# A small GpSimd write behind every fourth gather of a sparse graph attention

## The chip, the cores and the metric

The kernel runs on one core of one Trainium2 chip. The metric is the device time of one execution in microseconds (us). Lower is better. The engines are named as in the profile: PE is TensorE (PEld its weight loads), DVE is VectorE, ACT is ScalarE, POOL is GpSimd, SP is SyncE. [...]

## The reference, cut to what matters

Layer 0 is a graph attention of 8 heads over 4096 nodes with a 0/1 adjacency of about 32 neighbours per row; layer 1 takes three quantiles per feature over the kept neighbours of each node.

```python
Wh = jnp.einsum('nd,hde->hne', nodes, W)
e = leaky_relu(f1[:, :, None] + f2[:, None, :], 0.2)      # f1, f2: Wh times a1, a2
att = softmax(where(adj > 0, e, -9e15), axis=-1)
h = elu(jnp.einsum('hnm,hmd->hnd', att, Wh))
x = layernorm(nodes + elu(concat_heads(h) @ W1 + b1))
# layer 1, per node: drop some neighbours by rank, then
svals = sort(where(keep[:, :, None], x[None], big), axis=1)
agg = mean over q in (0.25, 0.5, 0.75) of svals[ceil(q * n_keep) - 1]
out = (0.5 * agg + 0.5 * x) @ W.T + b + x
```

## The kernel before, in words

The adjacency is turned into lists of neighbour indices (`neighbours`, `complete_records`), and nodes are sorted by their number of neighbours, so that a tile of 128 nodes (128 partitions) has lists of about equal length. The 32 tiles are worked in three blocks of 4, 9 and 19 tiles (`BLOCKS`). While the attention of one block runs, the lists of the next block are searched in small pieces between the attention's own instructions; the third block has no such search beside it, only the preparation of layer 1 in its last six steps. After all 32 tiles comes the quantile stage, called the sort stage below.

One call of `step` (L340) handles two tiles:

- `fetch_rows` (L818) issues the gathers of one tile. A tile has 24 to 64 slots, rounded up to a multiple of four, and each slot is one indirect DMA on POOL (`gather`, L177, recorded at L178) that brings a row of 136 floats for each of the 128 partitions. Sixteen slots share one buffer `G`, and the pool holds six of them (L829). Between the gathers stand some scatters (L187): the records of the next block, or `all_d` in the third block. `keep_x1` (L335) adds one scatter of finished rows per step.
- `attend` (L844) computes the attention of the tile before it. It is a chain over DVE, ACT and PE: logits `z` (L858, L864, exp at L865), denominators (L871, L881, L882), their spreading back (`rz`, L886, L895), block-diagonal weights `wide` of one layer of slots after another in two buffers (L902), one matmul per slot into `y` (L913), then the two dense layers in two halves of four heads (copies at L927, matmuls L934 and L948, ELU at L943, L945, L946) and the layer norm (`finish_x1`, L969). The last matmul into `y` that reads a `G` frees this buffer for later gathers.
- After the first part of `attend`, `prepare` reads the list of the next tile but one (`read_lists`, L767), whose transposed indices the next gathers need.

The order on each engine is the order in which the program issues (`manual_schedule`), and each engine takes its instructions in this order. A gather waits for its indices (DVE), for a free `G` (PE) and for the DMA that used its semaphore earlier. A matmul of L913 waits for its own gather.

Of the kernel before, what the change touches and what calls it, by code (L numbers as in the profile page):

```python
# [9 lines left out]
F32 = mybir.dt.float32  # L10
# [9 lines left out]
P = 128  # L20
# [156 lines left out]
def gather(nc, dst, rows, idx):  # L177
    nc.gpsimd.indirect_dma_start(  # L178
        out=dst,
        out_offset=None,  # L180
        in_=rows,
        in_offset=bass.IndirectOffsetOnAxis(ap=idx, axis=0),
    )


def scatter(nc, rows, src, idx):
    return nc.gpsimd.indirect_dma_start(  # L187
        out=rows,
        out_offset=bass.IndirectOffsetOnAxis(ap=idx, axis=0),
        in_=src,  # L190
        in_offset=None,
    )
# [9 lines left out]
def kernel(  # L202
# [137 lines left out]
    def step(fetch=None, soon=None, pieces=None, quota=0, first=False, among=()):  # L340
        if first:
            keep_x1(fetch)
        if fetch:
            weigh.append(fetch_rows(tc, attp, fetch, xt_d, list(among)))
        if not first:
            keep_x1(fetch)
        if len(weigh) > 1 or (weigh and not fetch):
            done = 0
            each = quota / STEPS
            for k, x1_t in enumerate(attend(tc, attp, pp, weigh.pop(0), consts)):  # L350
                if soon:
                    ready.append(prepare(*soon))
                    soon = None
                while done < min(quota, (k + 1) * each):
                    next(pieces, None)
                    done += 1
            store.append(x1_t)
            quota -= done
        if soon:
            ready.append(prepare(*soon))  # L360
        for _ in range(quota):
            next(pieces, None)
# [455 lines left out]
def fetch_rows(tc, ap, lists, xt_d, among):  # L818

    nc = tc.nc  # L820
    R, mine, parts = lists
    out = []
    left = sum(w for _, w, _, _ in parts)
    G, col = None, 16
    for s0, w, idx, f1v in parts:
        runs = []
        for g in range(w):
            if col == 16:
                G, col = ap.tile([P, 16, XW], F32, name="G", bufs=6), 0  # L829
            if not runs or col == 0:  # L830
                runs.append([G, col, g, 0])
            runs[-1][3] += 1
            gather(nc, G[:, col, :], xt_d, idx[:, g : g + 1])
            col += 1
            left -= 1
            if among and left % 2 == 0 and left <= 2 * len(among) + 4:
                scatter(nc, *among.pop(0))
        out.append((w, P // w, runs, f1v))
    for v in among:
        scatter(nc, *v)  # L840
    return R, mine, out
# [545 lines left out]
```

## Time and profile before

| | |
|---|---|
| median of 3 runs | 3876.51 us (3872.57 to 3877.78) |
| the profiled execution, its own time | 4780.24 us, span 4778.5 us |
| mean granted TensorE clock in it | 0.563 |
| POOL busy | 2763.5 us, 58% of the span, 2388 instructions |
| DVE busy | 2676.4 us, 56% |
| PE busy | 1355.3 us, 28% |
| gathers of the attention (`G`, L178) | 1180 indirect DMAs, mean 958 ns |
| gathers of the sort stage (`vals`, L178) | 1024 indirect DMAs, mean 1390 ns |

The profiled execution is 903.7 us longer than the median of the timed runs. Times in the lines of the trace are us from the span's start. In a line of the timeline the first number is the start, the second the duration, and the bracket gives the idle time of the engine before it and what ended this idle time; "issue" means that the profile shows nothing that was waited for, "remote" that it can't name the source. In a line of the groups the number after the `|` is the busy time in us, then the mean ns of one, then the idle time before the group and what ended most of it.

The attention's first gather starts at 113.9 us and its last at 2743.7 us; the sort stage's first gather starts at 2851.3 us.

### The profile page before, as it was taken

What the parts mean: (1) busy time and instruction counts of PE and PEld (TensorE: products, weight loads), DVE (VectorE), ACT (ScalarE), POOL (GpSimd) and SP (SyncE); (2) the same over time, 40 slices, a digit from 0 to 9 for tenths busy, and PEclk for the clock granted to TensorE, in tenths of its full rate; (3) what the DMA queues carried; (4) which work ended last, traced back from release to release, by engine and by line L of the source; (5) the groups of instructions that cost most, each with busy time, mean ns of one, the idle gap of its engine ahead of it and who ended that gap; (6) DMA issues with size and microseconds to landing.
All of it is one profiled execution on the core that took longest, in us unless ns stands there. A gap on an engine that the chain in (4) does not pass through costs nothing. (4 is left out here: it accounts for less than half of the span.)

```text
span 4778.5 us, 22122 instructions
## 1 busy us (share of the span) xinstructions
PE 1355.3 (28%) x5429; PEld 1026.7 (21%) x5433; DVE 2676.4 (56%) x6455; ACT 413.3 (9%) x667; POOL 2763.5 (58%) x2388
## 2 busy tenths in 40 slices
PE   5373445556233443343424250000000000000010
PEld 2042333333232342232423240000000000000010
DVE  7463354554313111111134235687779999999868
ACT  2110111211000101100000010000000000000000
POOL 1534434334544454544444518888878888888883
PEclk9995555555555555555555555555555555555555
DMA  5321323321111111111111101111111111111110
GB/s 182 113 72 40 115 77 95 99 79 47 45 42 35 37 41 35 39 36 39 43 36 31 40 8 43 40 40 37 39 41 41 37 30 33 41 40 37 36 40 20
DMA packets 110282, 241.26 MB, mean 50 GB/s; under 512 B 46976, under 2 KB 63360, under 8 KB 101952
## 3 DMA queue, kind: packets, MB, share of 16 engines
q0 software_dynamic: 76160, 160.24, 12.5%
q10 hardware_dynamic: 9360, 67.18, 4.1%
q1 hardware_dynamic: 24624, 12.34, 1.1%
q8 instruction: 45, 0.74, 0.1%
q14 instruction: 93, 0.76, 0.1%
HBM read 228.44 MB, written 11.15 MB: 50 GB/s over the span
## 5 line engine op out<-in xcount | busy, mean ns | idle before, releaser
L178 POOL DMA_INDIRECT G<-xt_d,idx x1180 | 1130.7, 958 | 1285.2 <-issue 692.4
L178 POOL DMA_INDIRECT vals<-x_d,idx x1024 | 1423.4, 1390 | 314.5 <-issue 303.2
L1113 DVE TENSOR_TENSOR work<-work 128x256 f32<-128x256 f32 (+7 forms) x1168 | 922.0, 824 | 0.7
L913 PE MATMUL y<-wide,G 128*128 128x32 f32 (+3 forms) x2360 | 540.2, 410 | 234.2 <-DVE wide L902 137.9
L1113 DVE TENSOR_TENSOR work<-work,work 128x512 f32<-128x512 f32 (+4 forms) x820 | 584.7, 739 | 1.3
L1133 PE MATMUL st_ps<-dg,goal 128*128 128x128 f32 x286 | 71.1, 425 | 1794.4 <-DVE goal L1113 1430.9
L913 PEld LDWEIGHTS y<-wide,G 128*128 128x128 f32 x2360 | 516.8, 328 | 267.4 <-DVE wide L902 150.1
L945 DVE TENSOR_SCALAR half<-half 128x512 f32<-128x512 f32 x64 | 27.6, 432 | 915.3 <-ACT half L943 822.3
L1133 PEld LDWEIGHTS st_ps<-dg,goal 128*128 128x128 f32 x286 | 63.0, 321 | 1800.4 <-issue 1799.5
L563 DVE MAX8 first<-key 128x8 f32<-128x128 f32 x1024 | 228.0, 283 | 300.9 <-remote 132.6
L1113 DVE TENSOR_TENSOR work<-vals 128x768 f32<-128x768 f32 (+11 forms) x64 | 128.8, 2028 | 269.6 <-DMA vals<-x_d,idx 266.0
L948 PE MATMUL small<-W_sb,half 128*128 128x128 f32 x512 | 120.8, 410 | 484.7 <-DVE half L946 315.7
L596 PE MATMUL key<-sgn,markb 128*128 128x512 bf16 x255 | 151.0, 593 | 254.1 <-DVE first L563 105.0
L948 PEld LDWEIGHTS small<-W_sb,half 128*128 128x128 f32 x512 | 102.9, 298 | 503.9 <-DVE half L946 331.0
L934 PE MATMUL hT<-half,W_sb 128*128 128x128 f32 x512 | 116.1, 400 | 236.3 <-ACT half L927 143.7
L557 ACT ACTIVATE sgn<-adj_t 128x2048 bf16<-128x2048 int32 x64 | 122.1, 1907 | 555.0 <-PE key L596 387.1
L927 ACT COPY half<-y 128x512 f32<-128x512 f32 x64 | 65.5, 1023 | 1073.7 <-remote 536.5
L934 PEld LDWEIGHTS hT<-half,W_sb 128*128 128x128 f32 x512 | 103.9, 301 | 252.0 <-ACT half L927 153.6
L886 PE MATMUL rz<-rden,ownT 4*128 4x32 f32 (+3 forms) x436 | 112.3, 434 | 152.8 <-DVE rden L882 113.8
L599 PE MATMUL key<-parts,oneb 64*128 64x512 bf16 x256 | 149.1, 583 | 9.0 <-POOL parts L196 6.3
L1132 ACT ACTIVATE dg<-ident,wt 128x128 f32<-128x128 f32 x143 | 47.5, 393 | 1092.5 <-PE st_ps L1133 1008.4
L886 PEld LDWEIGHTS rz<-rden,ownT 4*128 4x128 f32 x436 | 98.4, 322 | 170.9 <-DVE rden L882 124.6
(178 smaller groups left out, 1773.0 us busy)
## 6 DMA issues: line engine op xcount, KB each, us to landing
adj_t<-in_adj_dram ACTq DMA_DIRECT2D x64, 1024.0 KB
G<-xt_d,idx POOLq DMA_INDIRECT x1180
vals<-x_d,idx POOLq DMA_INDIRECT x1024
R<-rec_d SPq DMA_DIRECT2D x128, 26.2 KB
xt_d<-rec SPq DMA_DIRECT2D x4, 544.0 KB
rec<-in_x_dram SPq DMA_DIRECT2D x4, 512.0 KB
W_sb<-in_L_gnn_W_dram SPq DMA_DIRECT2D x2, 512.0 KB
a_b<-in_L_gnn_a_dram SPq DMA_DIRECT2D x2, 512.0 KB
```

The source lines that it names most:

```text
L178: nc.gpsimd.indirect_dma_start(out=dst, out_offset=None, in_=rows, in_offset=bass.IndirectOffsetOnAxis(ap=idx, axis=0),)
L557: nc.scalar.activation(sgn, adj_t, AF.Sign, accum_out=cnt[:, i : i + 1])
L563: nc.vector.max(first[:, ts(c0 // CW + c, 8)], key[:, ts(c, CW)])
L596: nc.tensor.matmul(key, lhsT=markb, rhs=sgn[:, ts(b, 512)], start=True, stop=False)
L599: nc.tensor.matmul(key, lhsT=oneb[0:64, :], rhs=parts[:, ts(r, 512)], start=False, stop=True)
L886: nc.tensor.matmul(rz[:, layer[i] * H : (layer[i] + w) * H], lhsT=ownT[w][:, r, :], rhs=rden.rearrange("p (g r h) -> p r g h", r=k // 4, h ...
L913: nc.tensor.matmul(yf[:, ts(g, c)], lhsT=G[:, col + g - g0, 0:D], rhs=pf[:, ts(g, c)], start=(i == 0 and g % (w // 2) == 0), stop=(i == le ...
L927: nc.scalar.copy(yT.rearrange("p h (u g) -> p g u h", u=4), yf.rearrange("p (g u h) -> p g u h", u=4, h=H)[:, :, :, h0 : h0 + 4],)
L934: nc.tensor.matmul(hT[:, ts(h, P)], lhsT=consts["W_sb"][:, h0 + h, :], rhs=yT[:, h, :], start=True, stop=True,)
L948: nc.tensor.matmul(o, lhsT=hv[:, h, :], rhs=consts["W1_sb"][:, h0 + h, :], start=(h0 + h == 0), stop=(h0 + h == H - 1),)
L1113: nc.vector.tensor_tensor(slots_of(dst, (j, c, s, m), size), slots_of(a, (i, c, s, m), size), slots_of(b, (i + d, c, s, m), size), op,)
L1133: nc.tensor.matmul(st_ps[:, u, :], lhsT=goal[:, (j * k + u) * D : (j * k + u + 1) * D], rhs=dg, start=(j == 0), stop=False,)
```

## The change

One instruction is added to the loop of `fetch_rows`: when the number of slots that are left of the tile is a multiple of four, POOL writes zeros to a tile of 128 partitions by 128 floats. The tile comes from the attention's pool with one buffer, and nothing reads it.

```diff
             gather(nc, G[:, col, :], xt_d, idx[:, g : g + 1])
             col += 1
             left -= 1
+            if left % 4 == 0:
+                nc.gpsimd.memset(ap.tile([P, 128], F32, name="pause", bufs=1), 0.0)
             if among and left % 2 == 0 and left <= 2 * len(among) + 4:
                 scatter(nc, *among.pop(0))
```

## The prediction, made before the changed kernel ran

> **What bounds the kernel now.** I read the page's second part first, for where in the span POOL is full: it is the only engine that gets added work.
>
> ```profile
> DVE  7463354554313111111134235687779999999868
> POOL 1534434334544454544444518888878888888883
> PEclk9995555555555555555555555555555555555555
> ```
>
> Up to slice 23 (the attention; the gathers run from 113.9 to 2743.7 us) POOL is busy four or five tenths of the time, in the sort stage eight. By these rows an added POOL instruction in the attention has room. But this execution took 4780.24 us, and the median of the timed runs is 3876.51 us: 903.7 us less. Where they go decides the case. The groups give POOL's work:
>
> ```profile
> L178 POOL DMA_INDIRECT G<-xt_d,idx x1180 | 1130.7, 958 | 1285.2 <-issue 692.4
> L178 POOL DMA_INDIRECT vals<-x_d,idx x1024 | 1423.4, 1390 | 314.5 <-issue 303.2
> ```
>
> The timeline of POOL shows the rhythm: 0.95 us of work, 0.30 us between, 1.25 us per gather, then a long gap to the next tile's first gather.
>
> ```profile
> 1556.73 0.94 POOL L178 DMA_INDIRECT G<-xt_d,idx  x1 [0.30 <-issue]
> 1557.98 1.00 POOL L187 DMA_INDIRECT x_d<-x_t,mine  x1 [0.30 <-issue]
> 1596.93 0.96 POOL L178 DMA_INDIRECT G<-xt_d,idx  x1 [37.95 <-issue]
> 1598.20 0.95 POOL L178 DMA_INDIRECT G<-xt_d,idx  x1 [0.30 <-issue]
> ```
>
> In the window of the gathers POOL has 1180 x 1.25 = 1475 us of them and 89 scatters x 1.31 = 117 us: 1592 of 2630 us. Some 1040 us are gaps, and these end when the chain of `attend` goes on. So I looked at the chain, in the timeline of all engines:
>
> ```profile
> 1628.21 0.37 PE L913 MATMUL y<-wide,G 128*128 128x128 f32 x1 [2.44 <-issue]
> ...
> 1642.39 1.22 DVE L902 TENSOR_TENSOR wide<-z,own 128x1024 f32<-128x1024 f32 x1 [28.34 <-remote]
> 1642.63 1.80 POOL L178 DMA_INDIRECT G<-xt_d,idx  x1 [5.12 <-remote]
> ```
>
> The third `wide` waits only until the first layer's matmuls have freed its buffer. The last recorded matmul of even the second layer ends at 1628.6 us, yet DVE, and POOL beside it, go on at 1642.4 us, released by nothing that the profile names. The timeline of ACT has more of such holds:
>
> ```profile
> 2183.63 0.44 ACT L865 ACTIVATE z<-z 128x288 f32<-128x288 f32 x1 [1.43 <-DVE z L864]
> 2212.09 1.02 ACT L927 COPY half<-y 128x512 f32<-128x512 f32 x1 [28.02 <-PE y L913]
> ...
> 2215.82 1.03 ACT L927 COPY half<-y 128x512 f32<-128x512 f32 x1
> 2244.34 0.60 ACT L943 ACTIVATE half<-hT 128x512 f32<-128x512 f32 x1 [27.49 <-issue]
> 2258.60 0.31 ACT L976 ACTIVATE ve<-v 128x128 f32<-128x128 f32 x1 [13.66 <-DVE v L974]
> ...
> 2263.43 0.44 ACT L865 ACTIVATE z<-z 128x288 f32<-128x288 f32 x1 [1.43 <-DVE z L864]
> ```
>
> ```profile
> 2761.12 0.50 ACT L865 ACTIVATE z<-z 128x352 f32<-128x352 f32 x1 [1.81 <-DVE z L864]
> ...
> 2801.52 0.60 ACT L943 ACTIVATE half<-hT 128x512 f32<-128x512 f32 x1 [3.13 <-PE hT L934]
> 2805.86 0.31 ACT L976 ACTIVATE ve<-v 128x128 f32<-128x128 f32 x1 [3.75 <-DVE v L974]
> ...
> 2810.89 0.42 ACT L865 ACTIVATE z<-z 128x256 f32<-128x256 f32 x1 [1.64 <-DVE z L864]
> ```
>
> From exp to exp (L865) the 36-slot step takes 79.8 us, but its second L943 waits 27.49 us where the late, unheld step waits 3.13, and its L976 13.66 where that one waits 3.75. Without these 34.3 us it is 45.5 us; the unheld step, of 44 slots, takes 49.8 us. The 903.7 us are 28.2 us for each of 32 steps, the size of the holds. **I read it so:** the holds belong to the profiled execution, and the timed attention runs with steps of about 45 us. Then POOL is close to full: 2630 - 904 = 1726 us for 1592 us of work, 92%. If part of the difference lies in the sort stage (at most the 266 us for which its DVE waits for `vals`), it is 1992 us and 80%.
>
> In the third block POOL has 708 slots x 1.25 = 885 us and 51 scatters x 1.31 = 67 us: 50.1 us per step against a chain of 45 to 50 us. There POOL sets the end. In the first two blocks DVE and PE also do the search, and the chain sets it.
>
> **What the Trainium skill says.** "GPSIMD Engine Reference", section 2.1, Instruction dispatch: the completion of a Pool instruction gates those who wait on its semaphore, and does not hold back the next one; each of eight cores goes on when its own share is done. "Perfetto Trace Analysis", section Per-engine timelines: descriptors are made on two of these cores, the recorded end is that of the last descriptor, and Pool instructions are to be timed from start to start. The trace agrees in so far as, at the kernel's start, the instruction of masks.py:199 begins at 1.10 us although L196 before it, begun at 1.00, lasts 0.13. "SBUF — State Buffer", section Who interferes with whom: a DVE instruction with two SBUF inputs contends with a GpSimd instruction that reads, not with one that only writes. The trace agrees for reads: beside L902 a gather takes 1.80 us instead of 0.95. A memset only writes; no run here shows that half.
>
> **The change, part by part.** Slots are multiples of four, so there are 1180 / 4 = 295 memsets: 41 in the first block (164 slots), 77 in the second (308), 177 in the third (708). In the built program nothing else moves: POOL's gathers and scatters keep their order and their waits, and PE, ACT and SP are the same; DVE has one more semaphore wait at the start of the sort stage, for the last memset, long done. Each memset waits for the memset before it, four gathers or 5 us earlier, long done: nothing. No engine waits for a memset inside the loop. The tile costs 512 bytes per partition and moves addresses: nothing. What is queued behind each memset is the next gather, and behind a tile's last memset the scatter of finished rows.
>
> The price: the kernel has one memset of the same shape, at its start.
>
> ```profile
> 0.75 0.20 POOL masks.py:197 MEMSET ident<- 128x128 f32 x1 [0.29 <-POOLq L1370]
> ...
> 1.00 0.13 POOL L196 IOTA pidx<- 128x1 f32 x1
> ```
>
> It takes 0.20 us, and the next instruction starts 0.25 us after it. Between two gathers no memset is shown. Bounds: 0 where the six cores without descriptors do their share during the gather and the others in the 0.30 us between; 0.20 + 0.30 = 0.50 us if a second such gap appears. A gain per memset has no reason in the trace. I take **0.25 us**, since start to start is what POOL's queue pays.
>
> On the path: in the third block 177 x 0.25 = 44 us, less its first four tiles (108 slots, 27 memsets, 7 us): those of 28 slots have three layers, so the chain (above 45 us) covers POOL (28 x 1.25 + 4 = 39 us). Remain 37 us. In the first two blocks 118 x 0.25 = 30 us lie beside the search's DVE and PE work; I put a quarter, 7 us, on the path, where POOL catches up after the waits for the ranks. The sort stage gets no memset and starts later by what the attention ends later. Sum 44 us: 3876.5 + 44 = **3921 us**. In a profiled execution the gaps of 20 to 40 us per step absorb most of it: 4780 us and 0 to 40 more.
>
> **The rivals.** A measurement of this kernel can tell about 0.2% (8 us) from no change.
>
> - *The chain covers the memsets* (not slower). If the timed POOL is quicker than the profiled one, the third block is bound by the chain. The point: a step has 37.3 slots, 2.7 scatters (3.5 us) and 9.3 memsets (2.3 us); with a chain of 45.5 us all of it hides once the gather's pitch is below (45.5 - 5.8) / 37.3 = 1.06 us. Against it: the pitch is a steady 1.25 us wherever nothing is waited for, and 903.7 us fit the holds. Also possible: the holds are real, and the difference is elsewhere; the gaps of 20 to 40 us then cover everything. Time: 3877 to 3884 us.
> - *The memset does nothing to POOL's pitch* (the change doesn't do what it says): 0 us each, 3877 us; counted with the case above.
> - *A full second gap*: 0.50 us each. The third block gives 150 x 0.50 = 75, the others 15 to 59: 3967 to 4010 us. For it: every POOL DMA has this gap. Against it: the memset at the start has 0.05 us.
> - *Faster*: the pauses keep gathers from colliding with L902. Each of its 64 instructions lengthens a gather by up to 0.85 us, 54 us if all vanished and the memsets were free: 3822 us. Against it: the gathers fill the rest of the time anyway, so a pause only moves the collision.
>
> **How the numbers follow.** POOL on the path at about 0.25 us: 0.60, 3895 to 3960 us. Full gap: 0.08. Covered or free: 0.20. Faster: 0.12. So slower 0.68, same 0.20, faster 0.12. The range from 3872 to 3985 us takes in the covered case and the first part of the full gap, and leaves out the faster case and the end of the dear one.
>
> **What would show it.** In the profile after: 295 rows of MEMSET `pause` on POOL of about 0.2 us; a start-to-start distance of 1.5 us between the gathers around one (1.25: free; 1.75: full gap); the holds on ACT unchanged; the rhythm of the sort stage unchanged. A profiled span that grows little beside timed runs that grow by 40 us would fit the reading of the holds; timed runs that do not grow would refute it, or the pitch.

## The result, and the profile after

The changed kernel takes 3891.50 us (median of 6 runs, 3886.22 to 3899.86). The kernel before takes 3878.24 us beside it. The ratio is 1.0039, interval [1.0029, 1.0049]: 13.3 us slower by the medians. The direction was right. The size was not: 44 us were forecast.

The profiled execution of the changed kernel took 3893.38 us, in line with its timed runs, and has none of the holds that the prediction discussed. The kernel before takes 3878 us on two of the chips used here and 4729 us in every execution on a third one, so runs are compared within a chip only, and traces only where the kernel before takes 3878 us. The kernel before was therefore profiled again on such a chip (span 3863.2 us), and the readings below compare these two traces.

Busy tenths in 40 slices, first of the kernel before in its second profile:

```profile
DVE  8774687773341322276346887679999999998788
POOL 1677655466677777777568888877788887888882
```

and of the changed kernel:

```profile
DVE  8774687773332322275346787679999999998789
POOL 1677656467777777777568888877888887888882
```

In the first profile of before POOL stood at four or five tenths in most of the attention. Here it stands at four to seven tenths in the first two blocks and at seven in most of the third, which is fuller, as the prediction had inferred for the timed runs. A row of seven tenths is also what a full POOL looks like in this kernel: 0.95 us of each 1.25 us count as busy, 76%.

The groups of the changed kernel on POOL (busy us, mean ns, idle before them and what ended it):

```profile
L178 POOL DMA_INDIRECT vals<-x_d,idx x1024 | 1411.4, 1378 | 314.4 <-issue 303.2 <-DMA vals<-x_d,idx 8.5 <-ACT halfid L437 2.4
L178 POOL DMA_INDIRECT G<-xt_d,idx x1180 | 1147.8, 973 | 450.0 <-issue 372.9 <-PE y L915 62.0 <-DVE f1x L809 6.4
L837 POOL MEMSET pause<- 128x128 f32 x295 | 67.2, 228 | 0.2
```

and of the kernel before in its second profile:

```profile
L178 POOL DMA_INDIRECT G<-xt_d,idx x1180 | 1148.3, 973 | 491.1 <-issue 399.4 <-PE y L913 68.9 <-DMA R<-rec_d 6.1
```

The 295 memsets have 67.2 us of work, and only 0.2 us of idle time stands before them. The idle time before the gathers falls from 491.1 to 450.0 us, while their own busy time stays (1148.3 and 1147.8 us). So the memsets took part of their time from the idle time of the gathers. The timeline of POOL in the changed kernel shows how:

```profile
1394.79 0.95 POOL L178 DMA_INDIRECT G<-xt_d,idx  x1 [0.30 <-issue]
1395.74 0.22 POOL L837 MEMSET pause<- 128x128 f32 x1
1396.12 0.95 POOL L178 DMA_INDIRECT G<-xt_d,idx  x1 [0.17 <-issue]
1397.38 0.95 POOL L178 DMA_INDIRECT G<-xt_d,idx  x1 [0.30 <-issue]
```

A gather waits 0.30 us after a gather. The memset does not: it starts where the gather's record ends, works 0.22 us, and the next gather follows after 0.17 us. From start to start the two gathers around a memset are 1.33 us apart instead of 1.25 (medians of 244 and 849 pairs: 1332 and 1253 ns). **The price of a memset is its own time + 0.17 - 0.30 us**, which is 0.08 us from the unrounded times, a third of the 0.25 us in the forecast.

Where this lands is read from stretches of the trace. Each row is one stretch with its length, then the busy time and count of PE, PEld, DVE, ACT and POOL, then clock, DMA share and GB/s. These are the last 15 of the third block's 19 tiles (first gather of the fifth tile to last gather), before and after:

```profile
1120.00:1895.00 775.00, 451.64 (x2074) 409.89 (x2074) 290.36 (x928) 103.97 (x138) 589.92 (x608) 0.54 0.25 57
```

```profile
1126.00:1914.00 788.00, 454.44 (x2074) 412.87 (x2074) 290.19 (x928) 103.98 (x138) 622.09 (x750) 0.54 0.23 56
```

PE, DVE and ACT have the same number of instructions, POOL has 142 more, which are the memsets, and the stretch is 13 us longer.

By the gathers in the traces the three blocks have 168, 336 and 676 slots, and so 42, 84 and 169 memsets; the forecast, and the expectations below, counted 41, 77 and 177. The table by stretch draws on seven profiles, these two and five of the experiments below, which leave the memsets out of some blocks. Each stretch goes from the first gather of its first tile to that of the next stretch (the last one to its own last gather). The times are the lowest and highest of the traces that have at most one memset in the stretch (four of them), and of those that have them as in the changed kernel (three); the difference is that of the means.

| stretch | memsets | without | with | difference | 0.08 us each |
|---|---|---|---|---|---|
| first block | 42 | 240.7 to 241.9 us | 240.4 to 241.1 us | -0.3 us | 3.4 us |
| second block | 84 | 603.2 to 605.5 us | 606.3 to 607.5 us | +2.6 us | 6.7 us |
| third block, first four tiles | 27 | 161.2 to 162.6 us | 158.6 to 163.6 us | +0.1 us | 2.2 us |
| third block, other 15 tiles | 142 | 773.0 to 776.9 us | 786.2 to 788.3 us | +12.3 us | 11.4 us |

The differences add up to 14.7 us, and nearly all of it lies in the last 15 tiles. The spans of the two profiles shown differ by more, 28.4 us; 10 us of that lie in the sort stage, whose length varies from trace to trace. In the traces without memsets there, where the kernel before takes 3878 us, it takes 1917 to 1934 us, and both ends of this range come from kernels with at most one memset.

### The profile page after: what moved, and what is told of

Same layout as the page of the kernel before. It is cut to its first block, busy times and chain, and to the rows that moved or that the text cites. A ratio compares the mean times of both kernels' runs of the same rounds, so it can differ in the third digit from the quotient of the medians.

```text
span 3891.6 us, 22422 instructions
## 1 busy us (share of the span) xinstructions
PE 1326.4 (34%) x5433; PEld 1005.9 (26%) x5433; DVE 2681.0 (69%) x6455; ACT 413.2 (11%) x667; POOL 2847.6 (73%) x2683
## 5 line engine op out<-in xcount | busy, mean ns | idle before, releaser
L178 POOL DMA_INDIRECT G<-xt_d,idx x1180 | 1147.8, 973 | 450.0 <-issue 372.9
L947 DVE TENSOR_SCALAR half<-half 128x512 f32<-128x512 f32 x64 | 28.5, 445 | 417.3 <-ACT half L945 417.3
L873 PE MATMUL small<-z,own 128*4 128x32 f32 (+3 forms) x436 | 59.6, 318 | 251.4 <-ACT z L867 251.4
L187 POOL DMA_INDIRECT out_dram<-o,own_i x32 | 69.8, 2182 | 82.9 <-ACT o L1161 59.6
```

What stands on the lines that cost most here:

```text
L178: nc.gpsimd.indirect_dma_start(out=dst, out_offset=None, in_=rows, in_offset=bass.IndirectOffsetOnAxis(ap=idx, axis=0),)
L187: return nc.gpsimd.indirect_dma_start(out=rows, out_offset=bass.IndirectOffsetOnAxis(ap=idx, axis=0), in_=src, in_offset=None,)
```

## The experiments

Theory A: POOL's queue sets the end of the third block, and of part of the first, and each memset costs that queue 0.08 us. Rivals: the new tile's place in memory, or the one longer wait at the sort stage (B), and that the first two blocks pay (C). A1 below is A with the price as a sum, the memset's time + 0.17 - 0.30 us. A memset is also called a pause, after its tile.

**Before, profiled again.** No edit.

> The kernel before, unchanged, profiled once more, to have its attention without the holds. If the holds belong to that one profiled execution, the span is now about 3877 us, POOL runs through the third block with hardly a gap above 0.5 us, and from gather to gather it takes 1.25 us. If the memset is what removes the holds from a profiled execution, the span is about 4780 us again.

It took 3864.97 us, span 3863.2 us, with no holds. ACT's timeline in it shows the step (exp to exp) and what ends it:

```profile
1392.47 0.42 ACT L865 ACTIVATE z<-z 128x256 f32<-128x256 f32 x1 [9.11 <-DVE z L864]
...
1443.17 0.44 ACT L865 ACTIVATE z<-z 128x288 f32<-128x288 f32 x1 [13.02 <-DVE z L864]
```

and the same step in the changed kernel:

```profile
1403.31 0.42 ACT L867 ACTIVATE z<-z 128x256 f32<-128x256 f32 x1 [9.72 <-DVE z L866]
...
1454.72 0.44 ACT L867 ACTIVATE z<-z 128x288 f32<-128x288 f32 x1 [14.50 <-DVE z L866]
```

This step grows from 50.7 to 51.4 us, and the wait of ACT at its end from 13.0 to 14.5 us. That the wait is in the end one for gathers is told by DVE's waits in the third block, first before, then after (us in total, times, longest):

```profile
DVE z L858 <- DMA G<-xt_d,idx: 75.8, 15, 13.6
```

```profile
DVE z L860 <- DMA G<-xt_d,idx: 85.5, 18, 14.1
```

The chain waits for gathers, 10 us more than before, though it is not held anywhere. POOL waits for next to nothing: over the last 15 tiles in the trace of before no idle time before one of its instructions is longer than 0.31 us. So its queue is full there. These 15 tiles take 775.3 us, 51.7 us each, beside the 50.1 us of POOL work per step in the forecast.

**The third block alone, and the first two alone.** The memset stands only where the block is the last, or only where it is not.

```diff
-            if left % 4 == 0:
+            if left % 4 == 0 and PAUSE[0]:      # set per block: last / not last
```

> Memsets in the third block alone, 177 of them. Theory A (POOL's queue sets the end of the third block, and a memset adds 0.08 us to the distance from gather to gather): 177 x 0.08 = 14 us, so 10 to 14 us more than before, nearly the whole change. Theory B (the moved addresses or the one longer wait at the sort stage cost the 13 us): 13 us as well. Theory C (the first two blocks pay): 0 to 5 us.

> Memsets in the first two blocks alone, 118 of them. Theory A: the first block's POOL has no gaps and pays 41 x 0.08 = 3 us, the second block's gaps of 12 to 33 us per step cover its 77: 0 to 4 us more than before. Theory B: 13 us. Theory C: 8 to 13 us.

Their memsets, counted in the trace (shortest, median and longest in ns, first and last start in us):

```profile
L839 POOL MEMSET pause<- x169: 218/223/469, 966.9 to 1912.9; 128x128 f32 x169
```

```profile
L839 POOL MEMSET pause<- x126: 218/223/484, 119.5 to 958.1; 128x128 f32 x126
```

The third block alone gave 3890.16 us against 3879.39 us, ratio 1.0029 [1.0017, 1.0041], +11 us. The first two gave 3880.94 us, 1.0008 [1.0000, 1.0017], +3 us by the ratio, +1.6 by the medians. Together that is the change, and C falls: the upper end of the second interval is below 7 us. Their traces give the third block 949.8 and 938.8 us (936.5 in the second profile of before). Which of the first two blocks pays was expected the wrong way round: with its memsets the first takes 241.1 us, as without, and the second 606.5 us.

**One memset only.** The tile is there, and is written once.

```diff
-            if left % 4 == 0:
+            if left % 4 == 0 and not PAUSE:
+                PAUSE.append(1)
```

> The same scratch tile in the same pool, written once instead of 295 times, so that the addresses move as in the changed kernel and POOL's queue is the old one. Theory A: 0 us (within 3 us). Theory B: 13 us more than before.

3879.21 us, 1.0003 [0.9989, 1.0017]: the tile's place in memory costs nothing that can be seen. B falls, as it did with the first two blocks alone, where it expected 13 us.

**Other sizes and densities, on the chip where before takes 4729 us.** Four kernels: 8 floats instead of 128, 512 bytes instead of 128 floats, a memset behind every gather, and (on the kernel before) one behind every fourth gather of the sort stage.

```diff
-                nc.gpsimd.memset(ap.tile([P, 128], F32, name="pause", bufs=1), 0.0)
+                nc.gpsimd.memset(ap.tile([P, 8], F32, name="pause", bufs=1), 0.0)
```

> The 295 memsets write 8 floats per partition instead of 128. Theory A1 (a gather starts 0.30 us after the gather before it, but only 0.17 us after a memset, so a memset of length m costs m + 0.17 - 0.30 us, and nothing when m is at most 0.13): m is about 0.11 us, so the distance from gather to gather stays at 1.25 us, and 0 to 4 us more than before. Theory A2 (each memset costs a fixed 0.08 us, whatever its length): 13 us more.

```diff
-                nc.gpsimd.memset(ap.tile([P, 128], F32, name="pause", bufs=1), 0.0)
+                nc.gpsimd.memset(ap.tile([P, 512], mybir.dt.uint8, name="pause", bufs=1), 0)
```

> The 295 memsets write 512 single bytes per partition instead of 128 floats, the same 512 bytes. If a memset takes time per element, as the one of 64x4096 bf16 at the start suggests (3.50 us, 0.85 ns each), m is about 0.53 us. Theory A1: 0.53 + 0.17 - 0.30 = 0.40 us each; with the 218 of the first and third block on the path 87 us, and some of the second block's 77 (up to 31 us): 85 to 110 us more than before. Theory A2, or a memset that takes time per byte: 13 us.

```diff
-            if left % 4 == 0:
-                nc.gpsimd.memset(ap.tile([P, 128], F32, name="pause", bufs=1), 0.0)
+            nc.gpsimd.memset(ap.tile([P, 128], F32, name="pause", bufs=1), 0.0)
```

> A memset of 128 floats behind every gather, 1180 instead of 295. Theory A1: 872 in the first and third block x 0.08 = 70 us, the second block's 308 mostly in its gaps (143 us in all): 65 to 80 us more than before. If POOL were not what sets the end there: far less.

```diff
                     gather(nc, vals[:, a : a + D], x1_d, idx[:, t, j : j + 1])
+                    if (j * k + u) % 4 == 3:
+                        nc.gpsimd.memset(sp.tile([P, 128], F32, name="pause", bufs=1), 0.0)
```

> No memset in the attention; the same memset behind every fourth gather of the sort stage (256), on the kernel before. POOL has no gap there, and a gather takes 1.71 us from start to start because DVE's two-input instructions hold it. Theory A1 with POOL setting the pace there: 256 x 0.08 = 20 us (15 to 25) more. Rival: DVE sets the pace and the memset, which only writes, runs while a gather would have been held anyway: 0 to 5 us.

| kernel | time (before 4728.97 us) | ratio |
|---|---|---|
| 8 floats | 4755.94 us | 1.0058 [1.0041, 1.0075] |
| 512 bytes | 4438.70 us | 0.9388 [0.9376, 0.9400] |
| every gather | 4509.94 us | 0.9521 [0.9495, 0.9547] |
| sort stage | 4795.30 us | 1.0151 [1.0138, 1.0164] |

These times missed the expectations of all theories. The traces of this chip have waits in the attention like those of the first profile, and two kernels were even faster than before. The pitch, the time from the start of one gather to the start of the next, can be read all the same. In the timeline of the kernel with 8 floats, gathers around a memset stand 1.25 us apart, as those without:

```profile
1390.70 0.94 POOL L178 DMA_INDIRECT G<-xt_d,idx  x1 [0.30 <-issue]
1391.65 0.12 POOL L837 MEMSET pause<- 128x8 f32 x1
1391.95 0.95 POOL L178 DMA_INDIRECT G<-xt_d,idx  x1 [0.19 <-issue]
```

0.12 + 0.19 is the 0.30 us that stands there anyway (medians of the pitch: 1249 ns with the memset, 1254 without): this memset is free for POOL's queue, and A2, the fixed price, falls. Why this kernel takes 27 us more on this chip is not explained, and it was not run where before takes 3878 us.

**The changed kernel, the wide one, the dense one and the sort stage once more.** No new edits; this time on a chip where before takes 3877.87 us.

> The changed kernel once more, beside the wide and the dense pause. If the kernel before takes about 3878 us here: theory A1 (the price is the memset's time + 0.17 - 0.30 us on POOL's queue, 0.08 us each; first and third block on the path) expects +11 to +16 us; theory H (only the chip decides, the pause itself costs nothing) expects within 8 us. If it takes about 4729 us here (a chip on which PE, ACT and DVE are held): A1 alone would still say 0 to +16 us; theory G (where there are holds, a slower rhythm of POOL shortens them) expects less than before, between the narrow pause (+27 us there) and the dense one (-219 us there), about -50 us.

> 512 bytes instead of 128 floats in each pause, a memset of 0.54 us. If the kernel before takes about 3878 us: A1 expects 0.54 + 0.17 - 0.30 = 0.41 us each, 218 of them in the first and third block = 89 us, and up to 31 us for the second block's 77: +85 to +120 us. Theory G without A1 (a slower POOL helps everywhere) expects less than before. If it takes about 4729 us: both expect what the run before showed, about -290 us.

> A pause of 128 floats behind each of the 1180 gathers. If the kernel before takes about 3878 us: A1 expects 0.08 us each, 872 of them in the first and third block = 70 us, and up to 25 us for the second block: +65 to +95 us. A price that the first pause of four pays and the others do not would give the +13 us of the change. If the kernel before takes about 4729 us: about -219 us, as before.

> No pause in the attention; instead one behind every fourth gather of values in the sort stage, 253 in all. If the kernel before takes about 3878 us: A1 expects 253 x 0.08 = 20 us; the run on the other chip had +66 us, 0.26 each. If that is the sort stage's own price it comes again (+55 to +75 us), if it was the holds it does not (+15 to +25 us).

| kernel | time | ratio | expected by A | measured |
|---|---|---|---|---|
| the change | 3892.58 us | 1.0035 [1.0020, 1.0049] | +11 to +16 us | +15 us |
| 512 bytes | 3949.28 us | 1.0190 [1.0173, 1.0207] | +85 to +120 us | +71 us |
| every gather | 3937.68 us | 1.0158 [1.0141, 1.0175] | +65 to +95 us | +60 us |
| sort stage | 3938.41 us | 1.0169 [1.0152, 1.0187] | +20 us | +61 us |

The timeline of the wide kernel has A's sum in one look:

```profile
1393.36 0.94 POOL L178 DMA_INDIRECT G<-xt_d,idx  x1 [0.30 <-issue]
1394.30 0.54 POOL L837 MEMSET pause<- 128x512 uint8 x1
1395.00 0.95 POOL L178 DMA_INDIRECT G<-xt_d,idx  x1 [0.17 <-issue]
```

1395.00 - 1393.36 = 1.64 us, 0.39 more than a plain pair (median over the trace 1648 ns, 0.40 more). By blocks the wide kernel is 5.8, 9.2 and 61.0 us longer than the second profile of before, for 42, 84 and 169 memsets of 0.40 us, which are 17, 34 and 68 us. The dense kernel is 2.6, 6.4 and 57.5 us longer, for 168, 336 and 676 memsets of 0.08 us: 13, 27 and 54 us. Both forecasts were too high because POOL has gaps of over 0.5 us that take up part of the price, in the first block too, which they let pay in full. In the trace of before these gaps are 13.8, 139.5 and 11.2 us in the three blocks; with the wide memset 1.6, 113.4 and 0.6 us remain, with the dense one 2.7, 119.5 and 6.6 us. The price less the gaps lost is 5, 8 and 57 us for the wide memset and 2, 7 and 49 us for the dense one, close to what was measured except for 8 us in the third block of the dense kernel.

The third block of before has one such gap, in its fourth tile, where POOL waits for ranks that DVE computes. First before, then the wide kernel:

```profile
1064.05 1.00 POOL L187 DMA_INDIRECT all_d<-rec,ranks  x1 [11.21 <-DVE ranks L739]
```

```profile
1077.42 1.01 POOL L187 DMA_INDIRECT all_d<-rec,ranks  x1 [0.64 <-DVE ranks L739]
```

So the first four tiles hide the 10.8 us of their 27 wide memsets but for 1.7 us, and the 8.6 us of their 108 dense ones but for 1.8 us. The other 15 tiles pay in full, 59.3 and 55.7 us for 57 and 45 us.

The price per memset is the same with one per four gathers and one per gather (pitch 1332 and 1334 ns), so it is not one that only the first pause of four pays. A "slower POOL helps everywhere" is refuted: what gained 290 us on the one chip costs 71 us on the other.

The sort stage costs more than A says, on both chips: 66 and 61 us for 253 memsets, 0.24 to 0.26 us each. It came again where nothing is held, so it is the sort stage's own price. The groups say where it sits. First the kernel before, then the one with the pauses in the sort stage:

```profile
L178 POOL DMA_INDIRECT vals<-x_d,idx x1024 | 1412.4, 1379 | 314.4 <-issue 307.4 <-DMA vals<-x_d,idx 4.0 <-ACT halfid L437 2.4
```

```profile
L178 POOL DMA_INDIRECT vals<-x_d,idx x1024 | 1456.8, 1423 | 281.1 <-issue 276.9 <-ACT halfid L437 2.4 <-DMA vals<-x_d,idx 1.6
...
L451 POOL MEMSET pause<- 128x128 f32 x253 | 56.5, 223 | 0.1
```

The memsets add 56.5 us and take 33.3 us of gaps: 23 us, A's price. The other 44 us are in the gathers, which have become longer themselves: 159 instead of 107 of them take 1.7 to 2.0 us. DVE's waits for them, in the sort stage, grow by 66 us:

```profile
DVE work L1113 <- DMA vals<-x_d,idx: 260.2, 10, 36.3
```

```profile
DVE work L1115 <- DMA vals<-x_d,idx: 326.2, 13, 39.5
```

That a shifted rhythm makes more gathers meet DVE's two-input instructions fits, and was not tested by itself. In the change under study this plays no part: its sort stage has the rhythm of before (a mean of 1688 ns from one gather of values to the next, against 1690).

## Why the prediction was right in direction and wrong in size

- **POOL is full in the third block of the timed runs: right.** It was inferred from an execution that did not show it. From its fifth tile on POOL has no gap above 0.31 us, and the chain waits for gathers. In the second profile of before the forecast's 1592 us of POOL work stand in 1780.8 us from first to last gather, 89%, where 92% or 80% were said.
- **The price of 0.25 us: the step that failed.** The mis-sized term is "start to start is what POOL's queue pays", taken from a memset followed by an IOTA; the distance between the gathers around a memset was to be 1.5 us, and is 1.33. Between two gathers the memset's own start to start is 0.39 us, even more, but the memset starts 0.30 us earlier than the next gather would have, so that only 0.08 us are added. With this term, and the memsets counted in the traces, the working of the forecast gives 142 x 0.08 = 11 us for the third block and 126 x 0.08 / 4 = 2.5 us for the first two, 14 us in all; 13.3 us and 15 us were measured. The forecast's lower bound named the 0.30 us as a place where the work might lie, but took it as all or nothing, and the forecast chose 0.25 us instead of adding up what would fit in there.
- **The slots by block: miscounted.** They are 168, 336 and 676, not 164, 308 and 708, so POOL's work in the third block is 48.0 us per step by the forecast's own sum, not 50.1. With the right counts that sum gives 43 us instead of 44; that the errors nearly cancel is luck.
- **Seven us off for the first four tiles of the third block: right, for another reason.** They hide nearly all of their memsets, which the wide and dense kernels show. The forecast let the chain of the short tiles cover POOL; the trace has POOL waiting once, 11.2 us for the ranks. At the measured price the discount is 2 us.
- **A quarter of the first two blocks on the path: about right**, +2.3 us by the table, +3 us by the ratio of the partial kernel, of 10 us. The quarter was a guess. It is the second block that pays, and the first that hides. Of the second block's +2.6 us, 1.8 lie in its last 42 gathers, behind a wait for ranks, the place that the forecast named.
- **"The holds belong to the profiled execution": right for the timed runs shown, wrong as a rule.** On one chip every timed execution of the kernel before has that length, 4729 us. Being profiled does not bring the holds: the second profile of before and all profiles of two chips are without them. The profiled span after was said to be 4780 us and 0 to 40 more; it was 3891.6 us, without holds. What the change does where the holds are was not run. On which chip the first profile of before was taken is not on record.
- **The rivals.** The covered case was out, since the pitch is 1.25 us and not below 1.06 us. A free memset was nearer than it looked: with 8 floats the pitch does not change. A full second gap is refuted; the gap after a memset is shorter, 0.17 us. Faster: in the changed kernel gathers still last up to 1.99 us beside L904 (L902 before), their busy time is the same within 0.5 us, and nothing was gained.

## What to carry to other kernels

Before pricing an instruction that is put between two others, look at what already stands between them: where each pair of a queue has a fixed gap, as here, the added work is charged against it, and the price is its own time plus the new gap less the old one. Then ask stretch by stretch whether the queue has gaps of its own to take up the rest; here the first block hid all of it and the last 15 tiles none. And ask whether the neighbours keep their length: in the sort stage they did not, and the same memset cost three times as much. And where one profiled execution is far from the timed runs, profile the same kernel again on another chip before arguing from either.

## What the runs showed of the hardware

- A memset on POOL starts at the recorded end of the gather before it, while a gather there waits 0.30 us. After the memset the next gather follows in 0.17 us, but not sooner than 0.30 us after the gather before: the pitch stays at 1.25 us with a memset of 0.12 us, and is 1.33 us with one of 0.22 us and 1.65 us with one of 0.54 us.
- A memset on POOL takes 0.12 us for 8 floats per partition, 0.22 us for 128 floats and 0.54 us for 512 single bytes. The last two write the same 512 bytes, so the time goes by elements and not by bytes: by the medians of 123, 224 and 543 ns it grows by 0.84 ns for each element from 8 to 128 and by 0.83 ns from 128 to 512.
- "SBUF — State Buffer", section Who interferes with whom, says that a DVE instruction with two SBUF inputs contends with GpSimd's reads and not with its writes, and that one in a two-port mode contends with GpSimd altogether. The changed kernel shows the half that was open: nine memsets lie wholly inside a write of `wide` (L904, two inputs, 1.22 us each) and take 0.22 to 0.23 us, as anywhere; in the dense kernel 48 do, with the same times. Beside L947, a tensor-scalar on one input, the five memsets that stand beside it for 0.25 us or more took 0.38 to 0.50 us, and each of them ended 0.14 us after L947 did. That would fit a memset that is shut out until L947 is done, and so the two-port mode; the trace does not name the mode, and gathers are hardly held there (29 with L947 wholly inside take 0.95 us in the median, 1.06 at most). One of the five, in the timeline of all engines of the changed kernel:

```profile
1751.03 0.42 DVE L947 TENSOR_SCALAR half<-half 128x512 f32<-128x512 f32 x1
1751.08 0.50 POOL L837 MEMSET pause<- 128x128 f32 x1
```

- The same program takes 3878 us on two chips and 4729 us on a third at the same granted clock (0.56), and there a slower POOL makes it shorter. In that chip's traces POOL's gaps of over 0.5 us between first and last gather are 975 us without memsets in the attention, 1031 us with those of 8 floats, 678 us with a memset behind every gather and 581 us with the wide one. Why PE, ACT and DVE are held there stays open, and so does what the change itself does there, which was not run.
